# A gated recurrence with its r and candidate sums in two PSUM banks of 32 columns, and another prologue

## The chip, the cores and the metric

The kernel runs on one core of a Trainium2 chip. The metric is the device time of one execution in microseconds; lower is better. PE is the matrix engine (PEld its weight loads), DVE the vector engine, ACT the scalar engine, POOL the GpSimd engine and SP the queue that starts most transfers. Matmul results land in PSUM, a small memory of eight banks of 512 f32 columns by 128 partitions; everything else lives in SBUF.

## What is computed

x is (8, 512, 256): 8 sequences, 512 time steps, 256 features, all f32; a condition vector of 256 features belongs to each sequence. Four layers follow each other, each added to x:

```python
x = x + L0(x, cond)   # shared gated MLP plus 8 experts, the best 2 per token by a router
x = x + L1(x, cond)   # reduces here to a factor for each sequence and feature
x = x + L2(x, cond)   # down, gelu, up, with low-rank parts generated from cond
x = x + L3(x, cond)   # a gated recurrence over the 512 steps
```

L3 is what orders the kernel. For every time step, with state h:

```python
z = sigmoid(x_t @ Wxz.T + bxz + h @ Whz.T + bhz)
r = sigmoid(x_t @ Wxr.T + bxr + h @ Whr.T + bhr)
c = tanh(x_t @ Wxh.T + bxh + (r * h) @ Whh.T + bhh)
h = z * h + (1 - z) * c
y_t = h @ Whq.T + bhq
```

Step t needs the h of step t - 1, so 512 steps run one after the other.

## The kernel before

**Blocks.** L0 to L2 work on blocks ("windows", w) of 32 time steps by 8 sequences, 256 columns; there are NW = 16. For each, `window_jobs` records jobs: the shared MLP (sw13, then sw2 into the PSUM tile acc), the experts (rw1, weighted by the router's gates bc, then rw2 into acc), x1 and x2 (L0's sum, then the factor of L1), and the "lower layers": two calls of `adapted` (base_down, then base_up, each with a low-rank part low_in and low_out), and at last xt, a copy of x with time outside, which the recurrence reads.

**Prologue.** Before the first step the weights are loaded on SP's queue in the order of the `load` calls, the condition's branch is computed (mean, hidden layer, low_in and low_out by `generate` from the eight pieces of w2), block 0 is done to its end and block 1 is begun. Two PSUM banks named grh hold the sums of r and c; the second, rh1, serves as scratch for the prologue (ring r_c) and is claimed, that is cleared by matmuls with zeros, at step 4.

**Loop.** Every step is written out by hand: the matmuls of r (`recur`) from the state s_h, ACT's sigmoid in two halves of 32 columns, DVE's transposes and product into s_rh, the matmuls of z, then those of c from s_rh, ACT's tanh in two halves, transposes and a scan that makes the new state. `across` issues each product as four matmuls side by side, one for each group of 32 partitions, with the state as weights and wh as the moving operand. `project` adds the x part, four steps at a time, in four pieces: r and c for one half of the features, z, and again; the pieces for r and c stand just before the s_rh matmuls of every second step. `biases` writes the bias rows of the next 16 steps into the bank that isn't in use.

**The order around it.** A planner fills the gaps. It keeps a clock of its own: STEP = 2.43 us for a step, TAKES for each job, MARGIN between engines, RATE and LAG for transfers. `jobs.run` emits the prologue by that clock; in the loop `first_slot` and `second_slot` say how many matmul jobs of the later blocks follow z's matmuls and c's matmuls, so that all of it is done by step LAST = 462. What the planner emits is a fixed order: on the chip each engine runs its own in that order and waits by semaphores. A matmul job ("quad" where it is one product) is four matmuls side by side, and each f32 matmul shows as two records in the profile.

In the program's order the first s_h matmul of a step stands behind all fillers of the step before it, and the fillers behind z.

Of the kernel before, what the change touches and what calls it, by code (L numbers as in the profile page):

```python
# [11 lines left out]
ALU = mybir.AluOpType  # L12
# [38 lines left out]
LOW = (3, 2), (0, 1)  # L51
EARLY = 4
# [9 lines left out]
AHEAD = 3  # L62
RATE = 0.40
LAG = 2.5
# [72 lines left out]
class Jobs:  # L137
# [42 lines left out]
    def run(self, until):  # L180

        while any(j.done is None for j in until):
            for eng, at in self.clock.items():
                if at <= self.now:
                    job = next((j for j in self.queues[eng] if j.ready(self.now)), None)
                    if job is not None:
                        self.queues[eng].remove(job)
                        job.emit(self.now)
                        self.clock[eng] = self.now + job.takes
            self.now += 0.02  # L190
# [10 lines left out]
def cond_resid_kernel(  # L201
# [73 lines left out]
    r_gl = ring("gl", [P, NT], 3)  # L275
# [7 lines left out]
    ps_g = pool_of("ps_g", 2, PSUM)  # L283
    ps_z = pool_of("ps_z", 1, PSUM)
    gz = ps_z.tile([P, 2, NG, FQ], F32, name="gz")

    def new_gates(c):
        rh = ps_g.tile([P, NG, 2, FQ], F32, name=f"grh_{c}", tag="grh")
        return rh, gz[:, c % 2]

    both = [new_gates(c) for c in range(2)]
    zeros = const.tile([P, NT], F32, name="zeros")
    nc.vector.memset(zeros, 0.0)
    rh0, rh1 = [g[0].rearrange("p n g f -> p (n g f)") for g in both]
# [17 lines left out]
    jobs = Jobs()  # L312

# [35 lines left out]
    def load_x(n, mb, some=None):  # L349

        if some is None:
            t0 = len(xw) * WS
            t = const.tile([P, KC, B, n * WS], F32, name=f"x{len(xg)}")
            xg.append((t0, t))
            xw.extend(t[:, :, :, ts(i, WS)] for i in range(n))
            some = (0, n)
        t0, t = xg[-1]
        a, b = (i * WS for i in some)
        for k in range(KC):
            got = load(t[:, k, :, a:b], xs[:, k, :, t0 + a : t0 + b], mb)  # L360
        got_x.extend([got] * (some[1] - some[0]))
# [4 lines left out]
    load_x(0, 0.25, (0, 1))  # L366
    sw13_sb = const.tile([P, 2, KC, HS], F32, name="sw13_sb")
    got_sw13 = [load(sw13_sb[:, g], rows_of(sw13[g]), 0.5) for g in range(2)]
    load_x(0, 0.4, (1, EARLY))
    got_vec = load(vec, vecs, 0, eng="ACT")  # L370
    got_b2 = load(b2[: 4 * R], bias2.rearrange("q (r d) -> (q r) d", d=C), 0, eng="ACT")
    rw1_sb = const.tile([P, KC, E, P], F32, name="rw1_sb")
    got_rw1 = load(rw1_sb.rearrange("p k e h -> p k (e h)"), rows_of(rw1), 1.0)
    sw2_sb = const.tile([P, HC, C], F32, name="sw2_sb")
    got_sw2 = load(sw2_sb, rows_of(sw2), 0.5)
    wsq_a = const.tile([P, KC, 5, C], F32, name="wsq_a")
# [5 lines left out]
    r_w2 = Ring(pro.enter_context(tc.tile_pool(name="w2q", bufs=5)), "w2", [P, R * C], 5)  # L382
    r_c = Ring(None, "c", None, 1, rh1)
    pieces = {}
    for pair_ in LOW:
        for k in range(KC):
            for q in pair_:
                z = Lazy(r_w2)
                pieces[q, k] = (z, load(z, w2[ts(k, P), ts(q, R * C)], 1.0, [z]))

# [76 lines left out]
    def window_jobs(w, routed, xt, via_pool=False):  # L467
# [18 lines left out]
        def fetch(i):  # L486
# [9 lines left out]
                [routed[w % EARLY]],  # L496
                [bcs[i]],
                1.0 if via_pool else None,
                lag=LAG,
# [27 lines left out]
        def hidden(lazy, n, lhs, got):  # L527
            last = None
            for k in range(KC):
                last = mm(  # L530
                    lazy,
                    n,
                    lambda k=k: lhs(k),
                    lambda k=k: x[:, k],
                    k == 0,
                    [last, got, got_x[w]],
                )
            return last
# [3 lines left out]
        for m in range(HC):  # L542
            h, sig, lin, g = bank(), Lazy(r_sig), Lazy(r_lin), Lazy(r_g)
            j1 = hidden(h, 0, lambda k, m=m: sw13_sb[:, 0, k, ts(m, P)], got_sw13[0])
            j3 = hidden(h, 1, lambda k, m=m: sw13_sb[:, 1, k, ts(m, P)], got_sw13[1])
# [26 lines left out]
        for e2 in range(0, E, 2):  # L572
            h = bank()
            for n in range(2):
                e = e2 + n
                j = hidden(h, n, lambda k, e=e: rw1_sb[:, k, e, :], got_rw1)
# [15 lines left out]
                    [h, sig, gl],  # L592
                )
# [15 lines left out]
        x1, x2 = Lazy(r_x1), Lazy(r_x2)  # L609
        done = []  # L610
        for m in range(KC):
            d = add(
                "DVE",
                lambda m=m: stt(
                    bt(x1.get()[:, m]), bt(acc.get()[:, m]), THIRD, x[:, m], ALU.mult, ALU.add
                ),
                [order[0]],
                [acc, x1],
            )
# [4 lines left out]
                        x2.get()[:, m].rearrange("p (b t) -> p b t", t=WS),  # L624
                        x1.get()[:, m].rearrange("p (b t) -> p b t", t=WS),
                        lr2[:, m, :].rearrange("p (b o) -> p b o", o=1).broadcast_to([P, B, WS]),
# [3 lines left out]
                    [x1, x2],  # L630
                )
            )

        def adapted(out, n, src, base, deps, first):

            lu = Lazy(r_m)
            last = None
            for k in range(KC):
                last = mm(
                    lu,  # L640
                    0,
                    lambda k=k: low_in[:, n, k, :],
                    lambda k=k: src.get()[:, k],
                    k == 0,
                    [*deps, got_low_in[n], last],
                    [src],
                    tiles=2,
                )
# [3 lines left out]
                    us[n][:BR].rearrange("p (b t) -> p b t", t=WS),  # L652
                    lu.get()[:BR, 0].rearrange("p (b t) -> p b t", t=WS),
                    own[:BR].rearrange("p (b o) -> p b o", o=1).broadcast_to([BR, B, WS]),
# [3 lines left out]
                [lu],  # L658
            )
            last = None  # L660
            for m in range(KC):
                for k in range(KC):
                    last = mm(
                        out,
                        m,
                        lambda k=k, m=m: wsq_a[:, k, base, ts(m, P)],
                        lambda k=k: src.get()[:, k],
                        m == 0 and k == 0,
                        [*deps, last],
                        [src],  # L670
                    )
            ends = []
            for m in range(KC):
                last = mm(
                    out,
                    m,
                    lambda m=m: low_out[:, n, ts(m, P)],
                    lambda: us[n],
                    False,
                    [masked, got_low_out[n], last],  # L680
                )
                ends.append(last)
            return ends

        mid_ps, mid = Lazy(r_low), Lazy(r_mid)
        ends = adapted(mid_ps, 0, x2, A_DOWN, done, True)
        mids = []
        for m in range(KC):
# [5 lines left out]
                    sig.get(), mid_ps.get()[:, m], AF.Erf, scale=0.5 * RSQRT2  # L694
                ),
                [ends[m]],
                [mid_ps, sig],
            )
# [4 lines left out]
                        mid.get()[:, m], sig.get(), 1.0, mid_ps.get()[:, m], ALU.add, ALU.mult  # L703
                    ),
                    [a],
                    [mid_ps, sig, mid],
                )
            )
        up_ps = Lazy(r_low)
        ends = adapted(up_ps, 1, mid, A_UP, mids, True)  # L710
        turned = []
        for m in range(KC):
            d = add(
                "DVE",
                lambda m=m: stt(
                    x[:, m], bt(up_ps.get()[:, m]), 0.25, bt(x2.get()[:, m]), ALU.mult, ALU.add
                ),
                [ends[m]],
                [up_ps, x2],
            )  # L720
            turned.append(
                add(
                    "POOL",
                    lambda m=m: nc.gpsimd.tensor_copy(
                        xt.get()[:, m], x[:, m].rearrange("p b t -> p t b")
                    ),
                    [d],
                    [xt],
                )
            )  # L730
# [15 lines left out]


# [43 lines left out]
    def route(ws, tiles, psum, via_pool, behind=()):  # L791
# [18 lines left out]
        for k in range(KC):  # L810
            deps = [*(got_x[w] for w in ws), got_rout_sq, *behind, d]
# [21 lines left out]
        def then(fn):  # L833
            nonlocal d
            queue = jobs.queues if via_pool else jobs.small
            d = jobs.add("DVE", fn, [d, got_rbias], (), takes, queue)
# [37 lines left out]
        made = []  # L874
        for i in range(n):
# [7 lines left out]
            made.append(jobs.add(eng, put, [d], (), 0.9 if eng == "POOL" else 0.5, lag=LAG))  # L883
# [4 lines left out]

    def mean_over_features(src, dep):
        ps = Lazy(r_c)  # L890

        def products():
            for k in range(KC):
                nc.tensor.matmul(
                    ps.get()[:, :B], inv_c, src[:, k, :], start=(k == 0), stop=(k == KC - 1)
                )

        return ps, pe(products, [dep], [ps])

    mu, j = mean_over_features(cond, got_cond)  # L900
    diff = set1.tile([P, KC, B], F32, name="diff")

    def center():
        for k in range(KC):
            tt(diff[:, k, :], cond[:, k, :], mu.get()[:, :B], ALU.subtract)

    j = dve(center, [j], [mu], 0.4)
    dsq = set1.tile([P, KC, B], F32, name="dsq")
    j = dve(lambda: tt(dsq, diff, diff, ALU.mult), [j])
    var_ps, j = mean_over_features(dsq, j)  # L910
    var = set1.tile([P, B], F32, name="var")
    j = dve(
# [568 lines left out]
```

## Time and profile before

| what | us |
|---|---|
| median of 3 runs (1319.23 to 1321.51) | 1320.2 |
| the profiled run | 1319.46 |
| its span, first to last instruction | 1317.7 |
| PE busy | 1182.9 (90%) |
| DVE busy | 914.0 (69%) |
| ACT busy | 507.2 (38%) |
| POOL busy | 149.3 (11%) |
| first r on ACT | 70.30 |
| last r on ACT | 1309.7 |

Busy time of the engines by stage (x stands for the number of instructions):

```profile
20.00:40.00 20.00, 18.36 (x296) 10.93 (x292) 10.54 (x47) 3.22 (x10) 5.65 (x10) 1.00 0.99 387
40.00:60.00 20.00, 19.33 (x334) 11.14 (x330) 6.02 (x25) 2.59 (x7) 6.05 (x10) 1.00 1.04 341
...
800.00:1000.00 200.00, 177.32 (x6065) 100.52 (x6065) 140.80 (x975) 80.26 (x545) 21.03 (x30) 1.00 0.06 17
```

The columns are the stretch, its length, the busy time of PE, PEld, DVE, ACT and POOL, the granted clock of PE, the share of the transfer engines that was busy and the GB/s. From 20 to 60 us PE and the transfers are both full; in the loop the transfers are nearly idle. A busy PE isn't PE at its peak: the records of matmuls that run side by side or after each other overlap, and a burst of several is shown as one row from its first start to its last end. In rows of the time line the two first numbers are the start and the length, "xN" the number of records merged, and what stands in brackets is the idle time before and what ended it. In the groups by form the numbers are the total busy time in us and the mean of one in ns.

### The profile page before, as it was taken

What the parts mean: (1) busy time and instruction counts of PE and PEld (TensorE: products, weight loads), DVE (VectorE), ACT (ScalarE), POOL (GpSimd) and SP (SyncE); (2) the same over time, 40 slices, a digit from 0 to 9 for tenths busy, and PEclk for the clock granted to TensorE, in tenths of its full rate; (3) what the DMA queues carried; (4) which work ended last, traced back from release to release, by engine and by line L of the source; (5) the groups of instructions that cost most, each with busy time, mean ns of one, the idle gap of its engine ahead of it and who ended that gap; (6) DMA issues with size and microseconds to landing.
All of it is one profiled execution on the core that took longest, in us unless ns stands there. A gap on an engine that the chain in (4) does not pass through costs nothing.

```text
span 1317.7 us, 88546 instructions
## 1 busy us (share of the span) xinstructions
PE 1182.9 (90%) x39016; PEld 682.1 (52%) x39016; DVE 914.0 (69%) x6255; ACT 507.2 (38%) x3403; POOL 149.3 (11%) x228
## 2 busy tenths in 40 slices
PE   8999999998999999998888888888888888888886
PEld 4565555555555555555554445554554545545443
DVE  4267777777767677776766767676676767667665
ACT  2133444443344444344444433444343444433332
POOL 3310101111010100101011010101101010110000
PEclk9999999999999999999999999999999999999999
DMA  9910001100010000101000010000001000000111
GB/s 336 344 46 13 4 4 54 36 14 28 5 44 12 20 21 13 44 4 36 5 20 20 13 28 4 28 12 21 21 4 36 4 4 4 4 4 5 36 32 24
DMA packets 41586, 46.44 MB, mean 35 GB/s; under 512 B 27472, under 2 KB 31088, under 8 KB 40048
## 3 DMA queue, kind: packets, MB, share of 16 engines
q1 hardware_dynamic: 38304, 38.31, 9.6%
q8 instruction: 305, 5.00, 1.6%
q0 software_dynamic: 1184, 2.31, 0.5%
q14 instruction: 81, 0.66, 0.2%
q10 hardware_dynamic: 1712, 0.16, 0.1%
HBM read 36.45 MB, written 4.33 MB: 31 GB/s over the span
## 4 chain that ended last, share of the span: by engine, by line
PE 67%; DVE 19%; ACT 9%; issue 4%; DMA 0%; ACTq 0%; DVEq 0%
PE grh L1117 36%; PE hp L455 11%; PE acc L455 7%; DVE d L1312 7%; DVE rT L1312 6%; ACT c L1298 5%; PE gz L1117 5%; ACT r L1298 4%; PE low L455 4%; DVE s_h L1388 3%; PE misc L455 3%; DVE s_rh L1329 2%; PE misc L1025 1%; DMA b<-in_bias_dram 0%; ACT sig L548 0%
## 5 line engine op out<-in xcount | busy, mean ns | idle before, releaser
L1298 ACT ACTIVATE r<-grh 128x32 f32<-128x32 f32 x1024 | 146.2, 195 | 426.6 <-PE grh L1117 426.6
L1312 DVE STREAM_TRANSPOSE rT<-r 128x32 f32<-128x32 f32 x1024 | 156.0, 190 | 220.7 <-ACT r L1298 217.1
L1117 PEld LDWEIGHTS grh<-wh,s_h 128*32 128x32 f32 x8192 | 139.9, 109 | 308.7 <-DVE s_h L1388 308.7
L1117 PE MATMUL grh<-wh,s_h 128*32 128x64 f32 x8192 | 221.2, 225 | 85.2 <-DVE s_h L1388 84.9
L1298 ACT ACTIVATE c<-grh 128x32 f32<-128x32 f32 x1024 | 146.3, 195 | 308.8 <-PE grh L1117 307.8
L1117 PE MATMUL grh<-wh,s_rh 128*32 128x64 f32 x8192 | 220.9, 225 | 35.3 <-DVE s_rh L1329 10.9
L1117 PEld LDWEIGHTS grh<-wh,s_rh 128*32 128x32 f32 x8192 | 138.7, 108 | 194.6 <-DVE s_rh L1329 190.8
L1312 DVE STREAM_TRANSPOSE d<-c 128x32 f32<-128x32 f32 x1024 | 156.5, 191 | 115.8 <-ACT c L1298 109.9
L1117 PE MATMUL gz<-wh,s_h 128*32 128x64 f32 x8192 | 208.9, 219 | 0.7 <-issue 0.6
L455 PE MATMUL hp<-x,sw_sb 128*32 128x256 f32 x2016 | 153.6, 387 | 1.7 <-ACT sig L548 1.6
L1117 PEld LDWEIGHTS gz<-wh,s_h 128*32 128x32 f32 x8192 | 152.8, 110 | 1.0 <-issue 1.0
L455 PE MATMUL hp<-x,rw_sb 128*32 128x256 f32 x2016 | 150.5, 380 | 1.5 <-ACT sig L580 1.1
L596 POOL TENSOR_TENSOR g<-gl,bc 128x256 f32<-128x256 f32 x128 | 93.6, 733 | 510.8 <-DVE s_h L1388 349.4
L455 PE MATMUL acc<-g,rw_sb 128*32 128x256 f32 x2048 | 150.8, 379 | 0.7 <-issue 0.7
L1388 DVE TENSOR_TENSOR_SCAN s_h<-d,d 128x16 f32<-128x16 f32 x1024 | 145.3, 184 | 0.0
L1329 DVE TENSOR_TENSOR s_rh<-rT,s_h 128x8 f32<-128x8 f32 x1024 | 133.1, 167 | 0.0
L1312 DVE STREAM_TRANSPOSE zT<-z 128x64 f32<-128x64 f32 x512 | 121.8, 238 | 0.6 <-ACT z L1298 0.5
L1298 ACT ACTIVATE z<-gz 128x64 f32<-128x64 f32 x512 | 121.3, 237 | 0.8 <-PE gz L1117 0.8
L1117 PE MATMUL grh<-wx,xt 128*32 128x128 f32 x2048 | 106.7, 274 | 1.3 <-ACT r L1298 1.3
L1402 ACT COPY hist<-s_h 128x16 f32<-128x16 f32 x512 | 106.2, 207 | 0.5 <-DVE s_h L1388 0.5
L1341 DVE TENSOR_TENSOR d<-zT,s_h 128x16 f32<-128x16 f32 x512 | 90.6, 177 | 17.5
L1342 DVE TENSOR_SCALAR d<-zT 128x16 f32<-128x16 f32 x512 | 86.4, 169 | 0.0
(151 smaller groups left out, 1190.9 us busy)
## 6 DMA issues: line engine op xcount, KB each, us to landing
bc<-comb_d SPq DMA_DIRECT2D x56, 256.0 KB, 3.2
w<-in_w_dram SPq DMA_DIRECT2D x8, 1024.0 KB, 12.8
out_dram<-x SPq DMA_DIRECT2D x14, 256.0 KB, 2.9
x<-in_xT_dram SPq DMA_DIRECT2D x2, 1536.0 KB
rw_sb<-in_rw_dram SPq DMA_DIRECT2D x2, 1024.0 KB
bc<-comb_d POOLq DMA_DIRECT2D x8, 256.0 KB, 6.8
sw_sb<-in_sw_dram SPq DMA_DIRECT2D x3, 512.0 KB, 6.4
wsq_a<-in_sq_a_dram SPq DMA_DIRECT2D x1, 1280.0 KB
```

Of the source, the lines that this page charges most:

```text
L455: nc.tensor.matmul(out[ts(j, 32)], lhs[:, ts(j, 32)], rhs, start=start, stop=False, skip_group_check=True,)
L596: lambda gl=gl, g=g, e=e: nc.gpsimd.tensor_tensor(g.get(), gl.get(), bcs[e // 2].get()[:, e % 2], ALU.mult),
L1025: nc.tensor.matmul(flat(gp)[ts(t, 32), :C], hid[:, r, k, :], w[:, ts(R // 2 * (t % 2) + r, C)], start=False, stop=False, skip_group_check= ...
L1117: nc.tensor.matmul(out[ts(j, 32)], lhs, rhs[:, ..., ts(j, FQ)], start=start, stop=False, skip_group_check=True,)
L1298: nc.scalar.activation(x, y, func)
L1312: ins = nc.vector.transpose(dst.rearrange("p i u b -> p i (u b)"), src.rearrange("p (i r) -> p i r", r=32),)
L1329: prod = tt(s_rh[u][:, k, u, :], rT[:, k, u, :], h[:, k], ALU.mult)
L1341: tt(d1[:, :, u, :, 1], zT[:, :, u, :], h, ALU.mult)
L1342: nc.vector.tensor_scalar(d0[:, :, :, 1], zT[:, :, u, :], -1.0, 1.0, ALU.mult, ALU.add)
L1388: new = nc.vector.tensor_tensor_scan(s_h[v][:, k, v].rearrange("p b w -> p (b w)"), d0[:, k].rearrange("p b w -> p (b w)"), d1[:, k, u].re ...
L1402: nc.scalar.copy(hist[:, :, t, :], s_h[v][:, :, v, :, 1])
```

## The change

**Banks.** grh becomes two tiles that stay for the whole run, one for each half of 32 outputs of every partition group, with room for two lots of 16 steps in each:

```diff
-    ps_g = pool_of("ps_g", 2, PSUM)
+    ps_g = pool_of("ps_g", 1, PSUM)
+    grh = [ps_g.tile([P, 2, NG, 2, 32], F32, name=f"grh{i}") for i in range(KC)]
     def new_gates(c):
-        rh = ps_g.tile([P, NG, 2, FQ], F32, name=f"grh_{c}", tag="grh")
-        return rh, gz[:, c % 2]
+        return [b[:, c % 2] for b in grh], gz[:, c % 2]
```

`across` takes the half; r and c are each computed by eight groups of four matmuls of 32 columns instead of four groups of 64, in the order state part 0 into half 0 and 1, state part 1 into half 0 and 1, and ACT reads half i from bank i. The x part for r and c goes by two matmuls of 64 columns where one of 128 stood. The bias rows go to one bank each, and the r matmuls that follow wait for the latest of these copies:

```diff
         def recur(out, g, s):
             made = []
             for k in range(KC):
-                made += across(out, s(k), wh[:, k, g])
+                if isinstance(out, list):
+                    for i in range(KC):
+                        made += across(out[i], s(k), wh[:, k, g], i)
+                else:
+                    made += across(out, s(k), wh[:, k, g])
             return made
...
-                made = recur(rh[:, n, 0], G_R, state(u))
+                pre_r, pre_h = [[b[:, n, i] for b in rh] for i in range(2)]
+                made = recur(pre_r, G_R, state(u))
                 for mm in made:
-                    implied(mm, *acted, *biased)
+                    implied(mm, *acted, *(b for b in biased if b is not rh_bias))
```

**Lower layers in two parts.** For the first two blocks (HALVED = 2) x1, x2 and the lower layers run over time steps 0 to 15 and then 16 to 31, two products to a job; the loop starts after the first half of block 0, and projections wait for the half that they read:

```diff
+        halves = 2 if w < HALVED else 1
+        for half in range(halves):
+            at = slice(half * WS // halves, (half + 1) * WS // halves)
+            turned.append(lower(w, at, acc, x1, x2, mid, xt, order[0]))
...
-        jobs.run(ends[0])
+        jobs.run(ends[0][0])
```

Blocks 2 to 15 keep their products. One of block 0's four half copies to xt goes to ACT.

**Prologue.** x of block 0 and sw13 are loaded by feature halves in turn, and the matmuls start with what is there; sw2 comes before rw1, which is loaded in two parts; the first three pieces of w2 are loaded into the space of x for blocks 4 to 15, so that x for those is loaded after `generate` has read them, and the ring for w2 has 4 instead of 5 buffers; the second block's gates are fetched only after the last piece of w2; the condition's mean and variance are recorded ahead of the router; the bank of rh1 is claimed before the loop instead of at step 4. The ring gl has 8 buffers instead of 3. The planner's constants: AHEAD 1 (was 3), RATE 0.36 (0.40), LAG 3.5 (2.5), and some takes; the small DVE jobs of the router also run in `jobs.run`:

```diff
-AHEAD = 3
-RATE = 0.40
-LAG = 2.5
+AHEAD = 1
+RATE = 0.36
+LAG = 3.5
...
-    r_w2 = Ring(pro.enter_context(tc.tile_pool(name="w2q", bufs=5)), "w2", [P, R * C], 5)
+    r_w2 = Ring(pro.enter_context(tc.tile_pool(name="w2q", bufs=4)), "w2", [P, R * C], 4)
+    x_rest = const.tile([P, KC, B, (NW - EARLY) * WS], F32, name="x1")
+    flat_x = x_rest.rearrange("p k b t -> p (k b t)")
+    lent = [
+        Ring(None, f"lent{n}", None, 1, flat_x[:, ts(n, R * C)])
+        for n in range(KC * B * (NW - EARLY) * WS // (R * C))
+    ]
...
-                z = Lazy(r_w2)
+                z = Lazy(lent[len(pieces)] if len(pieces) < len(lent) else r_w2)
...
+    z = Lazy(r_c)
+    marked = pe(lambda z=z: claim(z.get()), [got_low_in[1]], [z], 0.9)
```

STEP, LAST, MARGIN and LEAD stay.

## The prediction, made before the changed kernel ran

> **What bounds the kernel now.** I read the chain of waits first, then the time line of one step, then the groups by form, then the busy time by stage and the time line of the prologue and of the tail.
>
> ```profile
> span 1317.7 us, 88546 instructions
> ...
> PE 67%; DVE 19%; ACT 9%; issue 4%; DMA 0%; ACTq 0%; DVEq 0%
> ```
> The page: the chain that ends last is compute on PE, DVE and ACT; DMA has no share. One of the 512 steps, from the time line (start, length, both us):
>
> ```profile
> 600.78 0.43 PE L1117 MATMUL grh<-wh,s_h 128*32 128x64 f32 x16
> ...
> 601.03 0.41 PE L1117 MATMUL gz<-wh,s_h 128*32 128x64 f32 x16
> ...
> 601.28 0.29 ACT L1298 ACTIVATE r<-grh 128x32 f32<-128x32 f32 x2 [0.66 <-PE grh L1117]
> ...
> 601.51 0.30 DVE L1312 STREAM_TRANSPOSE rT<-r 128x32 f32<-128x32 f32 x2 [0.69 <-ACT r L1298]
> ...
> 601.76 0.26 DVE L1329 TENSOR_TENSOR s_rh<-rT,s_h 128x8 f32<-128x8 f32 x2
> ...
> 601.98 0.43 PE L1117 MATMUL grh<-wh,s_rh 128*32 128x64 f32 x16
> ...
> 602.48 0.29 ACT L1298 ACTIVATE c<-grh 128x32 f32<-128x32 f32 x2 [0.41 <-PE grh L1117]
> 602.70 0.30 DVE L1312 STREAM_TRANSPOSE d<-c 128x32 f32<-128x32 f32 x2 [0.24 <-ACT c L1298]
> 602.95 0.28 DVE L1388 TENSOR_TENSOR_SCAN s_h<-d,d 128x16 f32<-128x16 f32 x2
> ...
> 603.20 0.43 PE L1117 MATMUL grh<-wh,s_h 128*32 128x64 f32 x16 [0.25 <-DVE s_h L1388]
> ```
> The step is a ring of 603.20 - 600.78 = 2.42 us: PE burst to ACT 0.50, to DVE 0.23, to the product 0.25, to PE 0.22, and the same again for c (0.50, 0.22, 0.25, 0.25). 512 x 2.42 = 1239 us; the other 79 are the prologue (first r burst at 69.6), the tail (8) and a few late steps. So two things pay: a shorter ring, and an earlier first burst.
>
> ```profile
> L1117 PE MATMUL gz<-wh,s_h 128*32 128x64 f32 x8192 | 208.9, 219 | 0.7 <-issue 0.6
> L1117 PE MATMUL grh<-wx,xt 128*32 128x128 f32 x2048 | 106.7, 274 | 1.3 <-ACT r L1298 1.3
> L455 PE MATMUL acc<-g,rw_sb 128*32 128x256 f32 x2048 | 150.8, 379 | 0.7 <-issue 0.7
> L455 PE MATMUL hp<-hist,wh 128*32 128x128 f32 x608 | 48.5, 403 | 0.0
> ```
> The groups by form: an f32 matmul's length grows by (379 - 219)/192 = 0.83 ns per moving column. The last row, which reads hist with a stride, is 129 ns longer than the equal form above it, 1.0 ns per column.
>
> **The split of r and c, by one unknown.** Each matmul is two records, and four neighbours run side by side: a "quad". Before, a burst is four quads of 64 columns and both halves of r end with the last. After, it is eight quads of 32 in the order half 0, 0, 1, 1 (state part 0), then 0, 0, 1, 1 (part 1); PE signals after the sixth and after the eighth, and ACT's first half needs only the sixth. Let p be the pace from quad to quad. For 64 columns the gz row gives p: 410 - 219 = 191 ns of starts, of which 21 are the stagger inside a quad (four gz records in the tail take 0.24, so 240 - 219); 170/3 = 57. For half 0 the last quad starts after 5p instead of 3 x 57 = 171, and its record is 32 x 0.83 = 27 shorter. The change of each half ring is 5p - 198 ns: zero at p = 40. Half 1 ends after 7p, but ACT takes the halves some 93 apart (0.29 for two of 0.195), so it sets the ring, by 7p - 291, only from p = 46 on.
>
> For 32 columns the trace has only the tail's reads of hist:
>
> ```profile
> 1309.68 0.31 PE L455 MATMUL hp<-hist,wh 128*32 128x32 f32 x8
> ...
> 1311.95 0.69 PE L455 MATMUL hp<-hist,wh 128*32 128x32 f32 x32 [1.00 <-ACT hist L1402]
> ```
> With the group's 240 per record: two quads give 310 - 240 - 21 = 49, eight give (690 - 240 - 21)/7 = 61. From below, the columns alone: 57 - 27 = 30. So p lies between 30 and 61. The 61 contain the stride, 32 x 1.0 ns, and 61 - 32 = 29 is the lower bound again; wh and wx are read without a stride, as in the rows that fit 0.83. I take 32, just over the bound: 5 x 32 - 198 = -38 a half, -76 a step.
>
> The rule against it: the Trainium skill, TensorEngine Tiling (Array Packing), section Performance Considerations, says that a matmul costs about 60 cycles however few columns it has. By that rule p would stay 57, each half would lose 7 x 57 - 291 = 108 ns and PE's order some 39 a step, and the kernel would stand near 1447. No row of the trace before shows 32 unstrided columns.
>
> What PE gives back: the burst itself is longer, 8 x 32 - 4 x 57 = +28, and a projection piece becomes two of 64 columns for one of 128, 4 x 57 instead of 2 x (57 + 53) = +8. In every second step that piece and a filler stand right before the s_rh burst. So it stands before:
>
> ```profile
> 604.10 0.40 PE L1117 MATMUL grh<-wx,xt 128*32 128x128 f32 x8
> ...
> 604.39 0.43 PE L1117 MATMUL grh<-wh,s_rh 128*32 128x64 f32 x16
> ```
> The last record starts at 604.10 + 0.40 - 0.274 = 604.23 and streams 57 + 53 = 110 ns: PE is free at 604.34, the burst comes at 604.39, 50 ns of cover. The cover shrinks to 50 - 38 - 28 - 8 = -24: 24 ns in half the steps, 12 a step. Before the s_h burst the fullest steps have two fillers: c's 4 x 57 + 25 of start and 2 x 2 x 216 end 1117 after c's start, the burst comes 1220 after: 100 of cover for -38 and -28, so nothing. DVE order and count stay, and its transposes follow ACT's halves: nothing.
>
> The net is -64 ns a step, x 511 = -33 us. At p = 30: -96 + (50 - 48 - 12 - 8 = -18, so 9) = -87, -44 us. At p = 61: 7 x 61 - 291 = +136 a half, +272, and 50 + 136 - 260 - 8 = -82, so 41: +313, +160 us.
>
> **Biases in a shared bank.** ACT now writes the next 16 steps' biases into the banks that PE accumulates in, so the next r burst waits for that copy, and behind it on PE stand z and the fillers. The gz copy at 600.23 takes 0.40, to 600.63; the next burst is at 600.78: 0.15 of cover, 0.11 after. I take 0; without cover it is about 0.1 us in 62 steps, +6.
>
> **The prologue.** After acc ends (x1 on DVE at 54.11) PE is dense until the first burst:
>
> ```profile
> 54.11 0.76 DVE L614 SCALAR_TENSOR_TENSOR x<-acc,x 128x256 f32<-128x256 f32 x2 [0.62 <-PE acc L455]
> ...
> 66.60 1.21 POOL L724 COPY xt<-x 128x256 f32<-128x256 f32 x2 [10.80 <-DVE x L715]
> ...
> 69.62 0.32 PEld L1117 LDWEIGHTS grh<-wh,s_h 128*32 128x32 f32 x16
> ```
> Those 15.5 us hold the lower layers, two sides of 8 quads, 16 x 2 records x 0.216 = 6.9, and 16 quads of block 1, 6.9, beside the projections. By the new order the first half of the lower layers takes 3.5, a piece of the second half 0.7, block 1 has 9 quads, 3.9, and claiming the second bank, 0.9, moves here out of the loop: 15.5 - 3.4 + 0.7 - 3.0 + 0.9 = 10.7. But two more hp groups of block 1 stand before acc ends, 8 quads, 3.5. Summed over all matmuls up to the first burst, the order has 53.3 us of streaming against 54.3. So a dense PE brings the burst 1 us earlier; the rest depends on whether those groups fill waits. PE has 69.6 - 54.3 = 15 us outside streaming there, a good part in the first 20 us, which no edit fills. On SP, x for the later blocks now waits for three w pieces that borrow its space, and the second window's bc fetches for the last w piece: fewer bytes ahead of w, and block 4's x is read some 300 us later. Bounds -1 and -8; I take -4, since the fill is partial. AHEAD 1 instead of 3 is in that order. The other edits there (sw13 and rw1 loaded in other cuts, the condition's mean moved up, which drops one of ACT's 1.28 us table loads, longer rings, one more x load on SP's queue at 0.5) move no PE work, so I cost them inside these bounds. On POOL the four fetches now come after block 0's last product and before its x2, 4 x 0.55 = 2.2 us; its acc quads cover them, and if not, x2 is late by up to 2.2, which the bound of -1 holds.
>
> In the loop's first 32 steps the second halves add short ACT, DVE and POOL work; those steps already lose 32 x (2.468 - 2.417) = 1.6 us, and I add 1, bounds 0 and 4. The tail stays.
>
> Sum: 1317.7 - 33 - 4 + 0 + 1 = 1281.7 us of span. The profiled run took 1319.46, 1.8 more, and the median is 0.7 above it: **1284 us**.
>
> **Rivals.** A: the pace is short but PE's order eats it, as at p = 37: 5 x 37 - 198 = -13 a half, -26, and PE late by 50 - 13 - 68 - 8 = -39, so +20: -6 ns a step, -3 us, 1314 with the prologue. For it: PE is busy 90% and its cover is 50 ns. Against: the 30 from the columns. B, slower: 32-column quads run no faster than the tail's, 49 to 61. At 49: 7 x 49 - 291 = +52 a half, +104, PE late by 50 + 52 - 164 - 8 = -70, +35: +139 ns, +71 us, 1388; at 61, 1477. It decides from p = 38 on (-8 a half, -16, PE +21: +5 ns a step, which eats the prologue's gain). For it: the only rows of 32 columns. Against: their stride accounts for the excess. C: the halves don't come apart, since DVE runs transpose 0, 1, product 0, 1 in order and the second sets it: 1317 to 1320, the prologue alone. Against: half 1 is hidden behind ACT's 93.
>
> **How the numbers follow.** Forecast (1262 to 1300) 0.58, A with C (1300 to 1318) 0.20, B 0.20, no change 0.02. The low end is p = 30 with the prologue's 8: 1317.7 - 44 - 8 + 2.5 = 1268, less 6, since rows are rounded to 10 ns and p may be 1 lower; the high end takes in A and C: 1262 to 1318. The forecast's own range is 1262 to 1300. A measurement of this kernel tells 0.2% (2.6 us) from no change; so faster 0.77, same 0.03, slower 0.20.
>
> **What would show it.** Right: steps of 2.33 to 2.37, ACT r at 0.46 after PE, r bursts of 32 columns, x32, about 0.46 long, the first burst at 62 to 68. Wrong: rows of 32 columns whose quads stand 40 ns or more apart; idle PE before s_rh gone and DVE s_rh waiting long; a first burst past 69.

## The result, and the profile after

The changed kernel takes 1713.3 us, median of 4 runs (1707.27 to 1715.73), against 1320.4 for the kernel before on the same chip (4 runs): 1.2964 times as long, 95% interval 1.2947 to 1.2982. The forecast was 1284, the range 1262 to 1318.

The profiled run took 1715.47. Its page, the lines that answer to those shown of before:

```profile
span 1713.4 us, 125995 instructions
...
PE 1307.3 (76%) x57672; PEld 873.4 (51%) x57672; DVE 933.3 (54%) x6271; ACT 534.7 (31%) x3407; POOL 150.2 (9%) x235
...
q8 instruction: 450, 7.37, 1.8%
...
PE 66%; issue 21%; DVE 9%; ACT 4%; ACTq 0%
```

And two lines of the page of before, which the prediction did not use:

```profile
PE 1182.9 (90%) x39016; PEld 682.1 (52%) x39016; DVE 914.0 (69%) x6255; ACT 507.2 (38%) x3403; POOL 149.3 (11%) x228
...
q8 instruction: 305, 5.00, 1.6%
```

In the chain, "issue", time in which an engine waited for nothing that the profile shows, has gone from 4% to 21%, 360 us. PE is busy for a smaller share, yet has 57,672 x 2 = 115,344 records where it had 78,032. The queue line gives packets and megabytes: queue 8 moved 450 packets of 16 KB instead of 305. 115,344 / 450 = 256 records to a packet, and 78,032 / 305 = 256 as well: queue 8 brings PE's instructions, 256 at a time.

The time line shows what "issue" looks like. First the r half of a step without it, then its c half with it:

```profile
802.53 0.46 PE L1200 MATMUL grh<-wh,s_h 128*32 128x32 f32 x32
...
803.00 0.29 ACT L1392 ACTIVATE r<-grh 128x32 f32<-128x32 f32 x2 [0.63 <-PE grh L1200]
...
803.69 0.39 PE L1200 MATMUL grh<-wh,s_rh 128*32 128x32 f32 x23
...
804.79 0.28 PE L1200 MATMUL grh<-wh,s_rh 128*32 128x32 f32 x9 [0.71 <-issue]
...
805.05 0.29 ACT L1392 ACTIVATE c<-grh 128x32 f32<-128x32 f32 x2 [1.53 <-PE grh L1200]
```

The burst at 802.53 is what was forecast: 32 records in 0.46, ACT 0.47 after its start. The burst at 803.69 breaks off after 23 records; the other 9 come 0.71 after the last of those has ended, with no semaphore between them, and c starts 1.36 after the burst's start. Between 300 and 1200 us the trace of after has 232 such stops (over 0.25 us from one PE record's start to the next, released by nothing but "issue"), of 1.01 us (median). The starts of queue 8's packets around this place, from the trace (us):

```
fetch starts   ends      PE starts again   next fetch starts
798.91         799.97    801.32            802.37
802.37         803.35    804.79            805.94
```

PE starts again 1.35 and 1.44 us after a packet has landed, and the next packet is asked for 1.05 and 1.15 us after that. Over these stops the medians are 1.03 us for the packet, 1.39 from its end to PE's next record, 1.14 from there to the next fetch: 3.56 us for 256 records. A packet each 3.71 us is what the whole stretch shows, against one each 4.19 in the kernel before.

The places of the stops say the same without any times. If PE's instructions are numbered in the order of their starts (its few semaphore instructions counted with the records), 229 of the 232 stops stand at the same place: 193 instructions after a multiple of 256, so whole packets apart. The kernel before has two such stops in this stretch, both at 193.

The busy times of 300 to 1200 us, after and then before, have the same in records (the number behind x, PE then PEld):

```profile
300.00:1200.00 900.00, 682.29 (x30999) 458.38 (x30999) 494.93 (x3349) 289.57 (x1859) 73.28 (x105) 1.00 0.06 16
```

```profile
300.00:1200.00 900.00, 808.28 (x27480) 461.12 (x27472) 634.59 (x4399) 362.28 (x2460) 96.62 (x138) 1.00 0.06 17
```

61,998 / 900 = 68.9 PE records a us after, 61.1 before, at a granted clock of 1.00 in both. A step of before has 148 records there and ran in 2.42 us; a step of after has 222, and 222 / 68.9 = 3.22 us is its mean. So the theory, called "the supply" from here on: PE's instructions arrive at 69 a us at best, and the split, which makes r and c of twice as many matmuls, asks for more.

The groups by form, last column the idle time just before and what ended it, agree:

```profile
L1200 PE MATMUL grh<-wh,s_h 128*32 128x32 f32 x16384 | 279.7, 200 | 145.6 <-issue 87.8 <-DVE s_h L1484 39.6 <-DVE lin L591 1.0
L1200 PE MATMUL grh<-wh,s_rh 128*32 128x32 f32 x16384 | 279.2, 199 | 113.8 <-issue 103.3 <-DVE s_rh L1425 4.1 <-DVE d L1438 1.5
L1200 PE MATMUL gz<-wh,s_h 128*32 128x64 f32 x8192 | 246.1, 224 | 62.5 <-issue 61.6 <-ACT hist L1498 0.9
```

Even z's matmuls, whose form nobody changed, are preceded by 61.6 us of "issue"; in before that was 0.6.

### The profile page after: what moved, and what is told of

Same layout as the page of the kernel before. It is cut to its first block, busy times and chain, and to the rows that moved or that the text cites. A ratio compares the mean times of both kernels' runs of the same rounds, so it can differ in the third digit from the quotient of the medians.

```text
span 1713.4 us, 125995 instructions
## 1 busy us (share of the span) xinstructions
PE 1307.3 (76%) x57672; PEld 873.4 (51%) x57672; DVE 933.3 (54%) x6271; ACT 534.7 (31%) x3407; POOL 150.2 (9%) x235
## 3 DMA queue, kind: packets, MB, share of 16 engines
q0 software_dynamic: 1184, 2.31, 0.4%
## 4 chain that ended last, share of the span: by engine, by line
PE 66%; issue 21%; DVE 9%; ACT 4%; ACTq 0%
PE grh L1200 29%; PE hp L485 12%; PE gz L1200 9%; PE acc L485 7%; PE low L485 5%; DVE d L1406 5%; ACT c L1392 3%; PE misc L485 3%; DVE s_h L1484 2%; DVE rT L1406 1%; ACT r L1392 0%; PE misc L1104 0%; DVE s_rh L1425 0%; DVE zT L1406 0%; PE grh L1034 0%
## 5 line engine op out<-in xcount | busy, mean ns | idle before, releaser
L1200 PEld LDWEIGHTS grh<-wh,s_h 128*32 128x32 f32 x16384 | 219.4, 112 | 343.1 <-DVE s_h L1484 215.7
L1200 PE MATMUL grh<-wh,s_h 128*32 128x32 f32 x16384 | 279.7, 200 | 145.6 <-issue 87.8
L1200 PE MATMUL grh<-wh,s_rh 128*32 128x32 f32 x16384 | 279.2, 199 | 113.8 <-issue 103.3
L1200 PEld LDWEIGHTS grh<-wh,s_rh 128*32 128x32 f32 x16384 | 219.4, 111 | 229.2 <-issue 118.9
L1200 PE MATMUL gz<-wh,s_h 128*32 128x64 f32 x8192 | 246.1, 224 | 62.5 <-issue 61.6
L485 PE MATMUL acc<-g,rw_sb 128*32 128x256 f32 x2048 | 170.9, 384 | 11.2 <-issue 11.1
L485 PE MATMUL hp<-x,sw_sb 128*32 128x256 f32 x2016 | 166.9, 387 | 11.5 <-issue 10.3
L485 PE MATMUL hp<-x,rw_sb 128*32 128x256 f32 x2016 | 164.6, 383 | 9.2 <-issue 8.6
L1200 PEld LDWEIGHTS grh<-wx,xt 128*32 128x32 f32 x4096 | 115.8, 111 | 49.3 <-issue 24.5
L1200 PE MATMUL grh<-wx,xt 128*32 128x64 f32 x4096 | 126.1, 221 | 19.2 <-issue 19.2
```

The costliest lines, as they stand in the source:

```text
L485: nc.tensor.matmul(out[ts(j, 32)], lhs[:, ts(j, 32)], rhs, start=start, stop=False, skip_group_check=True,)
L1200: nc.tensor.matmul(out[ts(j, 32)], lhs, rhs[:, ..., j * FQ + at : j * FQ + at + n], start=False, stop=False, skip_group_check=True,)
```

## The experiments

Two rivals to the theory were kept. Banks: ACT and PE now meet in two shared banks all the time, and that costs. Prologue and planner: the halves, the new order and constants do it.

**z_split.** z's state product in halves, in its own single bank; everything else as before:

```diff
             for k in range(KC):
-                made += across(out, s(k), wh[:, k, g])
+                if k in (0, 1) and (g == G_ZH):
+                    for i in range(KC):
+                        at = slice(32 * i, 32 * i + 32)
+                        made += across(out[..., at], s(k), wh[:, k, g], i)
+                else:
+                    made += across(out, s(k), wh[:, k, g])
```

with `across` as in the change.

> The kernel before with one edit: z's state product, which no chain of a step waits for at once, goes as twice as many matmuls of 32 columns into the same bank: 32 more PE instructions in a step, 184 instead of 152; no second bank for r and the candidate, no other prologue. Theory (PE's instructions come too slowly; after got 224.5 a step in 3.204 us, 70 a us): 184 / 70 = 2.63 us a step, total 1400 to 1460, with PE gaps of 0.7 to 1.1 us inside bursts. Rival banks (ACT and PE meeting in two shared banks cost the time): 1320 within 5. Rival prologue and planner's constants: 1320 within 5.

1414.4 us, 1.0709 (1.0690 to 1.0729). Its busy times of 300 to 1200 us:

```profile
300.00:1200.00 900.00, 789.41 (x31285) 503.72 (x31284) 601.33 (x4118) 349.88 (x2302) 92.65 (x132) 1.00 0.06 18
```

69.5 records a us: the rate of after, in a kernel without its banks or its prologue. Both rivals had forecast 1320 within 5. All 103 stops of this kernel between 300 and 1200 us, counted as above, stand at 193 too.

**z_half_split.** The same with `if k in (0,) and (g == G_ZH)`.

> As the run that splits z's state product, but only for one of the two state parts: 16 more PE instructions in a step, 168. Theory of the supply: 168 / 70 = 2.40 us, just under the ring of 2.42, so 1318 to 1345 with few stalls. Both rivals: 1320 within 5.

1339.8 us, 1.0145 (1.0114 to 1.0176). The median step between 300 and 1200 us is still 2.417, the mean 2.451: at 164 records a step PE mostly gets its instructions and now and then doesn't (23 stops, all at 193).

**after_unsplit.** The changed kernel with 64 columns and 16 steps to a bank again:

```diff
-    grh = [ps_g.tile([P, 2, NG, 2, 32], F32, name=f"grh{i}") for i in range(KC)]
+    grh = [ps_g.tile([P, NG, 2, FQ], F32, name=f"grh{i}") for i in range(2)]
...
-        return [b[:, c % 2] for b in grh], gz[:, c % 2]
+        return grh[c % 2], gz[:, c % 2]
```

with `across`, `recur`, `project`, `biases` and `gate` as before.

> The changed kernel with r and the candidate again in matmuls of 64 columns, 16 steps to a bank, as before; the halved lower layers, the prologue and the planner's constants stay as changed. Theory of the supply: 152 PE instructions a step again, steps of 2.42, and only the prologue's gain is left: 1314 to 1319. Rival banks: the same. Rival prologue and planner: about 1700. It sizes the prologue's term, put at -4.

1319.1 us against 1320.7 for the kernel before, 0.9985 (0.9976 to 0.9994): without the split the loss is gone, which rules out the prologue and the planner as its cause.

**split_only.** The kernel before with the split alone; the only thing that moves into its prologue is the clearing of the second bank, from step 4.

> The kernel before with the two banks and the 32-column matmuls of r and the candidate alone; prologue, lower layers and planner's constants as before. Theory of the supply: 1700 to 1725, first r burst near 70, fetches of PE's instructions every 3.4 to 3.5 us in the loop. Rival banks: the same. Rival prologue and planner: 1285 to 1290.

1709.9 us, 1.2947 (1.2923 to 1.2971). The split alone makes 389 of the 393 us, so what else was changed makes next to nothing of the loss. The fetches come each 3.70 us, where 3.4 to 3.5 had been expected. As rivals, that leaves the banks.

**after_no_z.** The changed kernel, banks and all, with fewer matmuls elsewhere:

```diff
+                if g >= 2:
+                    parts.append(lambda: None)
+                    continue
                 parts.append(lambda k=k, xk=xk: across(z[:, n], xk, wx[:, k, G_Z]))
...
-                made_z = recur(z[:, n], G_ZH, state(u))
+                made_z = []
```

Here g counts the groups of four steps.

> The changed kernel without z's state product and, after the first two groups of steps, without z's x part, so its output differs: 40 PE instructions fewer in a step, 184.5, as many as the run that split z's state product in the kernel before (94,936 in all against its 94,424). The two shared banks, ACT's bias copies into them, the 32-column bursts, the prologue and the planner's constants all stay. Theory of the supply (one fetch of 256 PE instructions each 3.70 us at best, 69.2 a us): 2.6 us a step, 1395 to 1425, though nothing of the banks has changed. Rival banks: what the two banks cost stays, 1650 to 1715.

1418.8 us, 1.0748 (1.0716 to 1.0781). Nothing of the banks was touched, and 295 of the 393 us are gone; the rival had 1650 to 1715.

**late_split.** Only the second state part in halves, all in one bank: `if k in (1,) and (g != G_ZH)` in `recur`, on the kernel before.

> The kernel before with r and the candidate in 64-column matmuls for state part 0 and two halves of 32 for state part 1 only, all in the bank of before: half 0 then ends after 2 x 57 + 32 = 146 instead of 171 and its last record is 27 shorter, -52 ns a half ring, -104 a step, so steps without a stall of 2.31 to 2.33. 94,424 PE instructions. Theory of the supply: the mean step is 2.58 to 2.62 all the same, 1385 to 1420. If the supply did not bind: about 1270.

1413.7 us, 1.0710 (1.0689 to 1.0732): the third kernel with 94,400 to 94,900 PE records, and the third between 1413 and 1419. The forecast of its steps without a stall failed: 2.46, not 2.31 to 2.33. One burst and its ACT, from the time line:

```profile
1003.21 0.44 PE L1118 MATMUL grh<-wh,s_h 128*32 128x64 f32 x24 [0.25 <-DVE s_h L1394]
...
1003.73 0.29 ACT L1304 ACTIVATE r<-grh 128x32 f32<-128x32 f32 x2 [0.68 <-PE grh L1118]
```

ACT starts 0.52 after the burst (0.50 in before). In the trace only the last of the 24 records updates the semaphore that ACT's first half waits for; in the kernels with two banks the 24th of the 32 records does, and the last one again. So the halves came apart only where each had its bank, and here the longer burst just delays ACT.

**wide_fillers and late_split_wide.** A way to fewer instructions: a filler's four matmuls as one of 128 weight columns, alone and with the late split.

```diff
-        for j in range(tiles):
+        wide = tiles if tiles == NQ else 1
+        for j in range(tiles // wide):
             nc.tensor.matmul(
-                out[ts(j, 32)],
-                lhs[:, ts(j, 32)],
+                out[ts(j, 32 * wide)],
+                lhs[:, ts(j, 32 * wide)],
```

> The kernel before with every quad of a filler (four matmuls side by side of 32 weight columns and up to 256 moving columns) as one matmul of 128 weight columns: 63,328 PE instructions instead of 78,040, the same sums. Theory of the supply: 78,040 was not bound in the steady steps (a fetch each 4.19 us against 3.70 at best), so the ring of 2.417 stays, and only early steps can gain: 1312 to 1322, if one wide matmul takes no longer than its quad; if wide weight loads cost PE more, up to 1360.

> Both edits, the late split and the wide fillers: 79,712 PE instructions, near the 78,040 of before. Theory of the supply: no stalls beyond those of before, so the shorter ring counts: 2.31 to 2.34 a step, 1262 to 1285. If something else than the supply slows split bursts (a second matmul's start, ACT reading a bank that PE writes): 1320 or more.

1422.1 us, 1.0768 (1.0750 to 1.0786), and 1442.9 us, 1.0930 (1.0914 to 1.0946): both far off. The first has only 63,320 PE records and no lack of them (a packet each 5.47 us). From its time line:

```profile
801.00 1.13 PE L456 MATMUL acc<-g,sw_sb 128*128 128x256 f32 x4
...
801.61 0.28 DVE L1389 TENSOR_TENSOR_SCAN s_h<-d,d 128x16 f32<-128x16 f32 x2
802.06 0.43 PE L1118 MATMUL grh<-wh,s_h 128*32 128x64 f32 x16
```

Four wide records reach to 802.13, and the next burst starts 0.45 after the scan's start instead of 0.25 (602.95 to 603.20 in before). Its chain is 80% PE. The wide matmuls don't stream longer: the four start at 800.999, 801.319, 801.535 and 801.751, and 216 ns is also the pace of quads of 256 columns in before. The time is lost where the form changes: the first two wide starts stand 320 ns apart, and between 300 and 1200 us no s_h or s_rh burst starts less than 306 ns after a wide matmul (down to 166 after a filler of before). Whether that is the wide weight load or the change between tile sizes was not taken apart.

Of the 123 us that late_split_wide loses, 102 are the wide fillers' own. The late split adds 21 here, where PE's records come at 58 a us, but 94 to the kernel before, where it makes PE ask for more than 69. Its 0.05 us longer steps alone would make 25, which fits the supply. But fewer instructions in this form are no way out.

**after_no_z_no_x.** after_no_z with the x part of r and c left out too (for g from 2 on), so that the supply nearly suffices.

> The changed kernel without z's state product and without the whole x part after the first two groups of steps, so its output differs: 86,872 PE instructions, 183.5 a step in the first 32, 168 in the next 192, 163 in the next 256. Theory of the supply at 69.2 a us: 2.65, 2.43 and 2.36 a step, where 2.36 is also the split's own ring; with some stalls at that edge 1300 to 1325, most steps from 224 on at 2.355 to 2.365, under the 2.417 of before: the split's gain appears as far as the instructions come. Rival banks: what the two banks cost stays, over 1600.

1331.1 us, 1.0063 (1.0047 to 1.0080); 6 us above the range: 58 steps of over 2.6 us hold 37 us more than as many at the median. But 378 of its 511 steps are under 2.40, and the median between 300 and 1200 us is 2.362. From its time line:

```profile
1001.96 0.46 PE L1200 MATMUL grh<-wh,s_h 128*32 128x32 f32 x32 [0.26 <-DVE s_h L1487]
...
1002.43 0.29 ACT L1395 ACTIVATE r<-grh 128x32 f32<-128x32 f32 x2 [0.63 <-PE grh L1200]
...
1003.13 0.46 PE L1200 MATMUL grh<-wh,s_rh 128*32 128x32 f32 x32 [0.24 <-DVE s_rh L1428]
...
1004.33 0.46 PE L1200 MATMUL grh<-wh,s_h 128*32 128x32 f32 x32
```

1001.96 to 1004.33 is a step of 2.37, from two rows rounded to 10 ns. The split's gain is real where the instructions are there.

**unsplit_halved1 and unsplit_ahead3.** Two tries to keep more of the prologue's gain: after_unsplit with `AHEAD = 3` and `HALVED = 1`, and with `AHEAD = 3` alone.

> The changed kernel unsplit as in after_unsplit, with only block 0's lower layers in halves (HALVED = 1) and AHEAD = 3 as before: the first 32 steps of the loop hold 157.0 PE instructions each instead of 166.0 (products of 128 columns cost as many instructions as those of 256). after_unsplit began its loop 3.6 us earlier than the kernel before and lost 2.9 of it in those 32 steps, with stalls of PE for its instructions. Theory of the supply: most of that is kept, 1315 to 1318. If the loss there is other work (ACT, DVE, POOL of the second halves): 1318 to 1321.

> after_unsplit with AHEAD = 3 as before and both blocks still in halves: 165.0 PE instructions a step in the first 32. Theory of the supply: the loss in those steps stays, 1317 to 1321; tells which of the two edits of unsplit_halved1 counts.

1319.9 us, 0.9985 (0.9975 to 0.9994), and 1320.7, 0.9990 (0.9982 to 0.9999). The first missed the 1315 to 1318 of the supply and lies where the rival, other work, had put it; the second was as expected. after_unsplit began its loop at 66.73 (first r; 70.30 in before) and lost 4.5 us in the first 32 steps (1.6 in before); these begin at 69.19 and 67.45 and lose 2.6 and 5.2. What the first burst gains, the first steps give back for the most part in all three, and 0.10 to 0.15%, 1 to 2 us, is left.

In the traces the loss of these 32 steps goes with PE's stops in them (over 0.3 us from one record's start to the next, all at 193). before has none. after_unsplit has five of together 4.5 us and loses 2.9 more than before; unsplit_halved1 has three of 1.2 us and loses 1.0 more; unsplit_ahead3 has seven of 4.5 us and loses 3.6 more. So the stops are enough for these losses, though no run shows that each of them made its step longer.

The kernels that keep the fillers and the planner's settings of before or of after, in the order of PE's records (steps and packets between 300 and 1200 us; the shortest step of the whole run):

```
kernel            PE records   us      mean step   shortest   packet each
before            78,032       1320    2.420       2.412      4.19
after_unsplit     78,480       1319    2.422       2.408      4.19
z_half_split      86,224       1340    2.451       2.413      3.83
after_no_z_no_x   86,864       1331    2.429       2.351      3.78
z_split           94,416       1414    2.594       2.409      3.68
late_split        94,416       1414    2.600       2.451      3.69
after_no_z        94,928       1419    2.619       2.353      3.70
split_only        114,896      1710    3.199       2.355      3.70
after             115,344      1713    3.219       2.356      3.71
```

The shortest step depends on what was split and where; from 94,000 records on the time goes with their number, and the packets come each 3.7 us whatever the kernel does.

## Why the prediction was wrong

**The step that failed** is "What PE gives back: the burst itself is longer, 8 x 32 - 4 x 57 = +28", and its +8 for a projection piece. It costed the added matmuls by the time that they stream, as if their instructions were always there, and found 12 ns a step. Left out was a term for the supply: 72 more instructions in a step (32 each for r and c, 8 for the x part). By what the runs show it is 222 / 68.9 = 3.22 us of supply against a ring of 2.36, 0.86 us in each of the 511 steps, some +440 us on 1284, where +429 was measured. The row stood on the page of before: 305 packets for 78,032 records, one each 4.3 us of the span. That 3.7 is the floor no row of before told, but the count could have been priced as one more resource with a bound: the change asked for a packet each 256 / 222 x 2.36 = 2.7 us.

**Pace, p = 32: right.** In the unbroken part of the s_rh burst shown above the quads start at 803.745, 803.777, 803.809, 803.840 and 803.872. ACT comes 0.47 after the burst, forecast 0.46; steps without a stall take 2.356 to 2.362, forecast 2.353. The first burst starts at 67.76, inside the 62 to 68 that were to show the forecast right. So every sign that it named was there, in rows between the stops, and the time was wrong all the same. Rival B's mechanism, slow quads of 32 columns, did not happen: "slower" came true by luck, and 1713 lies far above B's highest, 1477. A and C did not happen either.

**The rule weighed there** (the Trainium skill, TensorEngine Tiling (Array Packing), Performance Considerations) would, by the prediction's estimate, have made p 57 and the time 1447; the 32 ns speak against it here, and the loss came from elsewhere. Another page speaks of what did bind: the Trainium skill, Runtime: NRT & Kernel Launch, Instruction fetch mechanics, says that engines refill their instruction memory in blocks of 16 KiB or 256 instructions, as queue 8 shows, and that the fetch is mostly hidden, since issue is slower than the refill. At 61 records a us it was, but for two stops between 300 and 1200 us; where more than 69 were asked for, it was not.

**Biases, 0, bound +6: some 5 us.** In after_no_z_no_x the step in which r waits for the first of the two bias copies (from the eighth step of each 16 to the ninth) has a median of 2.505 against 2.361 for most others, and the one two later one of 2.380: 0.16 us in each of 31 lots, 5 us. In the groups by form of that kernel, the idle time before PE's weight loads for r, its last part, names the releaser:

```profile
L1200 PEld LDWEIGHTS grh<-wh,s_h 128*32 128x32 f32 x16384 | 191.7, 112 | 301.5 <-DVE s_h L1487 250.3 <-ACT grh L1222 19.1 <-issue 13.8
```

19.1 us of PE's weight loads for r ended with ACT's copy into grh; the rows of before have no such releaser for r.

**The prologue, -4, bounds -1 and -8: right at its start.** The first r is 3.6 us earlier unsplit (66.73), 2.0 with the split (68.35): in after PE stops there too, in the middle of the first projections, as its time line shows:

```profile
66.48 0.32 PE L1200 MATMUL gz<-wx,xt 128*32 128x64 f32 x8 [2.12 <-issue]
```

**The first 32 steps, +1, bounds 0 and 4:** +2.9 unsplit, which takes most of the prologue's gain. Some of it is the same stall: step 0 takes 4.14 us, with PE stopped between two low-rank products (the time line of after_unsplit):

```profile
69.77 0.30 PE L485 MATMUL low<-u,low_out 128*32 128x128 f32 x1 [1.48 <-issue]
```

There the halves play a part, since a product of 128 columns has as many instructions as one of 256: 166 a step instead of 157 with block 1 whole. With 157, unsplit_halved1 lost only 1.0 more than before, but began later. How much of the +2.9 is the supply was not shown by an experiment; the five stops at 193, 4.5 us, leave room for all of it.

## What to carry to other kernels

Count instructions as well as busy time: divide the span by the packets of the engine's instruction queue, and ask what spacing the changed count would need. Cutting a matmul into narrower ones shortens a burst, but each piece costs as many instructions as the whole; the gain is there only while the new count still arrives in time, in the densest steps, not on average. "issue" in the middle of a burst, with no semaphore to wait for, is how the lack shows, and stops that stand a multiple of 256 instructions apart tell it from other causes: in wide_fillers, which lacks no instructions, the 57 "issue" stops between 300 and 1200 us share no such place.

## What the hardware showed unexpectedly

PE's instructions come no faster than a packet of 256 each 3.7 us in a sustained stretch, 69 a us, in all five kernels that ask for more, while PE starts records in a burst at 8 per 32 ns, some 250 a us. When it has run dry in after, it starts again 1.39 us after a packet lands (1.27 to 1.54 in 8 of 10 stops), and the next fetch begins 1.14 us after that, some 118 records on; the last record before the next stop starts 1.48 us after that fetch began, 0.38 after it landed. So the fetch is asked for too late to be hidden at this rate, and a round of fetch, landing and restart takes 3.56 us. In the stops of the other four kernels the restart (1.39 to 1.40 us after landing) and the time to the next fetch (1.14) are the same, though in the median 90 to 115 records start before that fetch.

Fillers as one f32 matmul of 128 weight columns held up this kernel by 7.7% against four side by side of 32, with a quarter of the instructions for them and the same 216 ns each once running. What cost the time were the changes of form around them.
